# A two-layer spectral convolution: in the mixing stage, the channels' sums and the mixing matmuls alternate in runs of 64 instead of 32

## The chip, the cores and the metric

One Trainium2 chip, of which the kernel uses one core. The metric is the device time of one execution in microseconds (us). The kernel before takes 2893.25 us, the median of three runs (2887.61 to 2897.32).

## The reference

The input x is 16 images of 16 channels of 256 x 256 in fp32. Two layers follow each other, both of the form x + conv(groupnorm(x)).

```python
x = x + _L0_conv_ref(_gn(x), L0_conv_weight)           # 3 x 3 circular convolution, 16 to 16 channels
x = x + _L1_conv_ref(_gn(x), ty, tx, pole1, pole2, residue)
# in _L1_conv_ref
alpha = fft2(x)
A  = 1 / (omega1 - pole1);  Bm = 1 / (omega2 - pole2)
S  = einsum('ikpq,oikp,xikq->oxik', residue, A, Bm)    # a 16 x 16 matrix for each of 256 x 256 frequencies
r1 = einsum('biox,oxik->bkox', alpha, S)               # mix the channels at each frequency
x1 = ifft2(r1).real
x2 = ...                                               # a transient part, from 4 x 4 sums over alpha
return x1 + x2 / Nx / Ny
```

The change concerns S and r1: the matrices S are sums over the poles p and q (here "the channels' sums"), and r1 applies them at each frequency (here "mixing").

## The kernel before

The kernel runs in stages, each with its own buffers. First the 3 x 3 convolution with its statistics (L224 to L284), then the forward transform of each image to half a spectrum, written to the scratch tensor aD in device memory; then the mixing stage (L815 to L1046), which reads aD and writes yD; last the inverse transforms along x and y with the transient part and the output. The change is in the mixing stage alone.

The mixing stage goes through 32 groups g of frequencies along x, each group with four of them and all 256 along the other direction. For each group there are three kinds of work.

- The channels' sums, `sums(kk, w)` (L902): 16 matmuls of 64 rows and 32 columns (array tile 64*32) on 256 columns, from the weights `w` and the constant table `ct`, into two PSUM tiles `ps_s`, the second of them for the odd half of the rows. The matmuls alternate between the two tiles. Eight calls, kk = 0 to 7, make the matrices of a group. Each tile is copied to the tile `sg` in SBUF (L1027), the first of a call by ScalarE and the second by VectorE. There are two `sg` buffers: while group g is mixed out of one, the sums of group g + 1 are written into the other (`ahead`).
- Mixing, `mix(n, sg, yt)` (L958): 8 matmuls with `sg` as the weights (array tile 128*64), on 128 columns of `abd`, the spectrum laid out in blocks, into one PSUM tile `ps_mix`. Sixteen calls make a group; four of them fill one output tile `yt` (L1032), three copied by ScalarE and the fourth by VectorE. Then the quarter of `abd` is loaded for the next group (`load`, L951, four transfers) and `yt` is stored (`store`, L979, four transfers). All of these transfers are issued on the SyncE queue, in program order. `abd` has a buffer for each quarter, `yt` has two buffers.
- The weights of the sums of later groups, `weights(g)` (L858): a generator of three steps. The first does three operations on VectorE (L866 to L873), the second three more with a reciprocal (L875 to L878), the third four (L881 to L884) and then one on GpSimd (L887), and returns the finished tile `wt`.

Each fp32 matmul and its weight load leave two records in the trace, so that 32 matmuls count as 64.

PSUM has eight banks of 128 x 512 fp32. In this stage four belong to `ps_s` (L826) and four to `ps_mix` (L827). A matmul that begins a tile waits until the copy that emptied its bank has ended; which of the four it gets was set at compile time.

The order of the work is written out by hand: the stage runs under `manual_schedule` (L1008), so that each engine executes its instructions as the loop L1016 to L1042 issues them. The loop goes over four quarters n of a group. A quarter is: two calls of `sums` for the next group (32 matmuls), the four copies of their tiles, four calls of `mix` (32 matmuls) with their copies, load, store, and one step of the weights. In the last group (g = 31) there are no sums left. After group 2, `unmix_first` (L986) takes one of the two `yt` buffers to correct the first slot of yD, and gives it back in group 3 after quarter 1.

Of the kernel before, what the change touches and what calls it, by code (L numbers as in the profile page):

```python
# [9 lines left out]
FP = mybir.dt.float32  # L10
# [6 lines left out]
B = 16  # L17
C = 16
N = 256
P = 128  # L20
# [4 lines left out]
def conv_then_laplace_kernel(ctx: ExitStack, tc: tile.TileContext, a: dict, out: bass.AP):  # L25
# [15 lines left out]
    nc = tc.nc  # L41
# [173 lines left out]
    sums = tp.tile([P, 2, B, 12], FP, name="sums", tag="sums")  # L215
# [376 lines left out]
    for g in range(24 * B + 3):  # L592
# [3 lines left out]
        b, n = divmod(g, 24)  # L596
# [24 lines left out]
    def pool(stage, name, bufs=1, **kw):  # L621
        return stage.enter_context(tc.tile_pool(name=name, bufs=bufs, reuse_waits="tile", **kw))
# [17 lines left out]
    m, n = cols[:, 16:17], cols[:, 17:18]  # L640
# [177 lines left out]
    yp = pool(p2, "yt", 2)  # L818
# [10 lines left out]
    def new_sg(g):  # L829
        return (g0, g1)[g % 2].tile([P, N, 2 * C], FP, name="sg", tag="sg")  # L830
# [27 lines left out]
    def weights(g):  # L858

        shape = [P, 32, 4]
        u = up.tile([P, 4, 32, 4], FP, name="u", tag="u")
        w, den, e, f = (u[:, j] for j in range(4))
        pr2, pre, pim = (prU[:, j].unsqueeze(2).to_broadcast(shape) for j in range(3))
        nc.vector.tensor_tensor(  # L866
            w,
            omg[:, g].unsqueeze(1).to_broadcast(shape),
            pims.unsqueeze(2).to_broadcast(shape),
            ALU.subtract,  # L870
        )
        nc.vector.tensor_tensor(den, w, w, ALU.mult)
        nc.vector.tensor_tensor(den, den, pr2, ALU.add)  # L873
        yield
        nc.vector.reciprocal(den, den)  # L875

        nc.vector.scalar_tensor_tensor(e, w, m1, pre, ALU.mult, ALU.add)
        nc.vector.scalar_tensor_tensor(f, w, nm0, pim, ALU.mult, ALU.add)  # L878
        yield
        v = up.tile([P, 32, 2, 2, 4], FP, name="v", tag="v")  # L880
        nc.vector.tensor_tensor(v[:, :, 0, 0], e, den, ALU.mult)  # L881
        nc.vector.tensor_tensor(v[:, :, 1, 1], e, den, ALU.mult)
        nc.vector.tensor_tensor(v[:, :, 1, 0], f, den, ALU.mult)
        nc.vector.tensor_scalar(v[:, :, 0, 1], v[:, :, 1, 0], -1.0, None, ALU.mult)  # L884
        wt = wp.tile([P, 4, 8, 2, 32], FP, name="w", tag="w")
        full = [P, 64, 4, 8]
        nc.gpsimd.tensor_tensor(  # L887
            wt.rearrange("p a k o (i m) -> p (a k o) i m", i=4),
            v.rearrange("p a o r s -> p (a o) (r s)").unsqueeze(2).to_broadcast(full),
            m4.unsqueeze(1).unsqueeze(3).to_broadcast(full),  # L890
            ALU.mult,
        )
        return wt

    def at_once(steps):
        while True:
            try:
                next(steps)
            except StopIteration as e:
                return e.value  # L900

    def sums(kk, w):  # L902

        ps = [pg.tile([P, 2, N], FP, name="ps_s", tag="ps_s") for _ in range(2)]
        for ro in range(2):
            for iq in range(4):
                for odd in range(2):
                    rows = slice(64 * odd, 64 * odd + 64)
                    nc.tensor.matmul(  # L909
                        ps[odd][32 * iq : 32 * iq + 32, ro],  # L910
                        lhsT=w[rows, iq, kk, ro],
                        rhs=ct[rows, iq, kk],
                        start=True,
                        stop=True,
                    )
        return ps

    def first_sums():

        wt, w128 = at_once(weights(0)), at_once(weights(32))
        sg = new_sg(0)
        other = up.tile([P, 2, 2 * C], FP, name="other", tag="other")
        for kk in range(8):
            for h, w in enumerate((wt, w128)):
                fy = slice(P * h, P * h + P)
                ps = sums(kk, w)
                for odd in range(2):
                    k = slice(4 * kk + 2 * odd, 4 * kk + 2 * odd + 2)  # L930
                    copy = (nc.scalar.copy, nc.vector.tensor_copy)[odd]
                    copy(sg[:, fy, k], ps[odd][:, :, fy].rearrange("p r n -> p n r"))
                    copy(other[:, 1 - h, k], ps[odd][:, :, P * (1 - h)])
        for h in range(2):
            o, d = sg[:, P * h], other[:, h]
            nc.vector.tensor_tensor(d, d, o, ALU.subtract)
            nc.vector.scalar_tensor_tensor(o, d, fixrow, o, ALU.mult, ALU.add)
        return sg

    def finish_projections():  # L940


        accs = up.tile([P, 2, B, 16], FP, name="accs", tag="u")
        nc.vector.tensor_tensor(accs, proj[:, :, :, :, 0], proj[:, :, :, :, 1], ALU.add)
        for ro in range(2):
            ps = pm.tile([P, B, 16], FP, name="ps_o", tag="ps_mix")
            nc.tensor.matmul(ps, lhsT=jmat[:, 0], rhs=accs[:, ro], start=True, stop=False)
            nc.tensor.matmul(ps, lhsT=jmat[:, 2 - ro], rhs=accs[:, 1 - ro], start=False, stop=True)
            nc.vector.tensor_copy(o2[:, :, ro], ps)

    def load(g, jq):  # L951
        for s in range(4):
            nc.sync.dma_start(
                out=abd[jq][s::4, s].rearrange("r c j b -> r c (j b)"),
                in_=aD[4 * g + s].rearrange("r (c h n) -> r c h n", c=4, h=4)[:, :, jq],
            )

    def mix(n, sg, yt):  # L958


        ps = pm.tile([P, 4, 2, 4, B], FP, name="ps_mix", tag="ps_mix")
        jq = n // 4
        for j in range(4):
            cc, jj = divmod(4 * (n % 4) + j, 8)
            for t in range(2):
                f = 128 * t + 64 * cc + 16 * jq + 2 * jj
                nc.tensor.matmul(  # L967
                    ps[64 * t : 64 * t + 64, j],
                    lhsT=sg[:, f : f + 2].rearrange("p f m -> p (f m)"),
                    rhs=abd[jq][:, :, 2 * t + cc, 2 * jj : 2 * jj + 2].rearrange(  # L970
                        "p s j b -> p j s b"
                    ),
                    start=True,
                    stop=True,
                )
        j0 = 4 * (n % 4)
        return yt[:, :, :, j0 : j0 + 4], ps.rearrange("p j o s b -> p o (s b) j")

    def store(g, jq, yt):  # L979
        for c in range(4):  # L980
            nc.sync.dma_start(
                out=yD[4 * g : 4 * g + 4, :, c, jq].rearrange("s k n -> k s n"),
                in_=yt[32 * c : 32 * c + 32, c % 2].rearrange("p (s b) j -> p s (b j)", s=4),
            )
# [24 lines left out]
    ahead = first_sums()  # L1009
# [3 lines left out]
    wt = at_once(weights(1))  # L1013
    finish_projections()
    unmix = None
    for g in range(32):  # L1016
        sg, w_now = ahead, wt
        steps = weights(g + 2) if g < 30 else iter(())
        ahead = new_sg(g + 1) if g < 31 else None
        for n in range(4):  # L1020
            evict = []
            if ahead is not None:
                evict = sums(2 * n, w_now) + sums(2 * n + 1, w_now)
            yt = yp.tile([P, 2, 4 * B, 16], FP, name="yt", tag="yt")
            for j, ps in enumerate(evict):
                k = 4 * n + j
                (nc.scalar.copy, nc.vector.tensor_copy)[j % 2](  # L1027
                    ahead[:, :, 2 * k : 2 * k + 2], ps.rearrange("p r n -> p n r")
                )
            for m in range(4):  # L1030
                o, src = mix(4 * n + m, sg, yt)
                (nc.vector.tensor_copy if m == 3 else nc.scalar.copy)(o, src)  # L1032
            if g < 31:
                load(g + 1, n)
            store(g, n, yt)
            if n == 1 and unmix is not None:
                next(unmix, None)
                unmix = None
            try:
                next(steps)  # L1040
            except StopIteration as e:
                wt = wt if e.value is None else e.value  # L1042
        if g == 2:
            unmix = unmix_first()
            next(unmix)
# [152 lines left out]
    for n, (k, b0) in enumerate(units):  # L1198
# [12 lines left out]
        r = rp.tile([P, 2, 4, N], FP, name="r", tag="r")  # L1211
# [163 lines left out]
```

## Time and profile before

From the page of the profile; span 2897.0 us, granted clock 0.965 in the mean over the kernel.

| | busy us | share of the span |
|---|---|---|
| TensorE, matmuls | 2667.3 | 92% |
| TensorE, weight loads | 1971.8 | 68% |
| VectorE | 1940.5 | 67% |
| ScalarE | 1536.0 | 53% |
| GpSimd | 1003.5 | 35% |

| group of instructions | count | busy us | mean ns of one |
|---|---|---|---|
| L967, mixing matmul, 128*64, 128 columns | 8192 | 479.4 | 276 |
| L909, matmul of the sums, 64*32, 256 columns | 8448 | 260.6 | 382 |
| L1027, copy of sums to sg, ScalarE | 248 | 159.9 | 646 |
| L1032, copy of a mix to yt, ScalarE | 384 | 221.6 | 587 |
| L1032, copy of a mix to yt, VectorE | 128 | 88.6 | 692 |

Matmuls of one kind run several at a time in the array, so that the mean of one is longer than the busy time divided by the count. The mixing stage lies between about 1410 and 2130 us of the span, a quarter of the whole. PE is TensorE's matmuls and PEld its weight loads, DVE is VectorE, ACT is ScalarE, SPq the SyncE queue. In a timeline, a line has the start and the length in us, the engine, the line of the kernel, the operation with the tiles it writes and reads, and in brackets the idle time of the engine just before and what ended it.

### The profile page before, as it was taken

How to read it: one execution, taken by the hardware profiler on the slowest of the kernel's cores; microseconds unless marked ns; L12 is line 12 of the kernel's file. 1: busy time of each engine (PE TensorE's matmuls, PEld its weight loads, DVE VectorE, ACT ScalarE, POOL GpSimd, SP SyncE). 2: the span in 40 equal slices, each digit the busy share in tenths (PEclk: the TensorE clock that was granted, in tenths of full speed). 3: DMA queues.
4: the chain of work that ended last, by engine and by line, in shares of the span. 5: the costliest groups of instructions: out<-in, count | busy, mean ns of one | idle time of the engine just before them, and what ended most of it. 6: DMA issues, size and time to landing. Idle time of an engine off the chain costs nothing.

```text
span 2897.0 us, 92787 instructions
## 1 busy us (share of the span) xinstructions
PE 2667.3 (92%) x39536; PEld 1971.8 (68%) x39536; DVE 1940.5 (67%) x3572; ACT 1536.0 (53%) x3098; POOL 1003.5 (35%) x906
## 2 busy tenths in 40 slices
PE   4878878889799999997899999999969999999998
PEld 2333334346577777775688888888868888888887
DVE  7766698886788888887444444444427666766666
ACT  3556677667466666664345555555524444444443
POOL 2232566420233333333211111111135554555553
PEclk9989998899899999998899999999989999999999
DMA  6555667665566666664466666666679999888995
GB/s 257 203 179 187 212 238 256 229 240 192 182 211 211 233 233 224 227 218 169 150 193 191 191 196 193 193 192 191 190 212 312 285 285 288 285 284 285 290 288 188
DMA packets 477335, 650.63 MB, mean 225 GB/s; under 512 B 49065, under 2 KB 458665, under 8 KB 462969
## 3 DMA queue, kind: packets, MB, share of 16 engines
q1 hardware_dynamic: 472920, 635.37, 67.0%
q8 instruction: 312, 5.11, 0.7%
q10 hardware_dynamic: 3408, 7.34, 0.7%
q0 software_dynamic: 592, 1.97, 0.3%
q14 instruction: 103, 0.84, 0.1%
HBM read 365.09 MB, written 279.45 MB: 222 GB/s over the span
## 4 chain that ended last, share of the span: by engine, by line
PE 56%; DMA 9%; DVE 6%; SPq 2%; POOL 1%; issue 1%; ACT 0%; DVEq 0%; ACTq 0%; POOLq 0%
PE ps_mix L967 15%; PE ps_s L909 8%; PE ps_y L678 8%; PE ps_y L686 8%; DMA yk<-yD 4%; PE ps_x L721 4%; PE ps_p L1148 4%; PE ps_f L1157 3%; PE ps_f L1158 3%; DMA out_y<-ol 3%; DVE r L1166 2%; PE psd L706 1%; DVE ol L1168 1%; DVE ol L1169 1%; SPq L1099 1%; DMA yD<-yt 1%
## 5 line engine op out<-in xcount | busy, mean ns | idle before, releaser
L238 PE MATMUL ps_conv<-xt,wc 32*32 32x512 f32 x12288 | 477.4, 641 | 18.0 <-ACT vt L255 11.2
L967 PEld LDWEIGHTS ps_mix<-abd,sg 128*64 128x64 f32 x8192 | 448.5, 138 | 65.5 <-ACT sg L1027 49.8
L967 PE MATMUL ps_mix<-abd,sg 128*64 128x128 f32 x8192 | 479.4, 276 | 13.4 <-ACT yt L1032 13.4
L1112 POOL TENSOR_TENSOR u<-yk 128x512 f32<-128x512 f32 x256 | 342.2, 1366 | 369.8 <-PE ps_p L1148 241.6
L694 ACT ACTIVATE t<-ps_y,vmr 128x384 f32<-128x384 f32 x512 | 297.7, 582 | 168.4 <-PE ps_y L686 157.0
L238 PEld LDWEIGHTS ps_conv<-xt,wc 32*32 32x32 f32 x12288 | 231.8, 106 | 214.8 <-issue 142.1
L1032 DVE COPY yt<-ps_mix 128x512 f32<-128x512 f32 x128 | 88.6, 692 | 363.8 <-PE ps_mix L967 231.8
L678 PE MATMUL ps_y<-tabE,vq 128*128 128x256 f32 x1024 | 313.1, 387 | 13.9 <-DVE vq L667 12.2
L887 POOL TENSOR_TENSOR w<-v,mcol 128x2048 f32<-128x2048 f32 x33 | 119.3, 3614 | 583.8 <-DVE v L884 580.8
L1157 PE MATMUL ps_f<-pt,inv 128*128 128x256 f32 x1024 | 305.8, 380 | 0.0
L686 PE MATMUL ps_y<-tabO,vq 128*128 128x256 f32 x1024 | 305.7, 380 | 0.0
L1158 PE MATMUL ps_f<-hs,ey 128*128 128x256 f32 x1024 | 305.0, 379 | 0.0
L1032 ACT COPY yt<-ps_mix 128x512 f32<-128x512 f32 x384 | 221.6, 587 | 147.2 <-PE ps_mix L967 95.8
L1148 PEld LDWEIGHTS ps_p<-inv,u 128*128 128x128 f32 x2048 | 265.1, 192 | 49.2 <-issue 24.3
L1148 PE MATMUL ps_p<-inv,u 128*128 128x128 f32 x2048 | 278.1, 279 | 12.6 <-POOL u L1115 12.5
L909 PE MATMUL ps_s<-ct,w 64*32 64x256 f32 x8448 | 260.6, 382 | 27.1 <-DMA ct<-cD 27.1
L1161 DVE TENSOR_TENSOR r<-ps_f,q 128x256 f32<-128x256 f32 x256 | 107.2, 419 | 252.1 <-ACT q L1160 252.1
L255 ACT ACTIVATE vt<-ps_conv,xq 128x512 f32<-128x512 f32 x256 | 167.1, 680 | 194.0 <-PE ps_conv L238 193.0
L1027 ACT COPY sg<-ps_s 128x512 f32<-128x512 f32 x248 | 159.9, 646 | 199.7 <-PE ps_s L909 199.5
L678 PEld LDWEIGHTS ps_y<-tabE,vq 128*128 128x128 f32 x1024 | 189.5, 190 | 90.3 <-ACT q L734 50.3
L1160 ACT COPY q<-ps_f 128x256 f32<-128x256 f32 x256 | 95.4, 373 | 290.8 <-PE ps_f L1158 290.8
L909 PEld LDWEIGHTS ps_s<-ct,w 64*32 64x32 f32 x8448 | 158.4, 107 | 92.3 <-POOL abd L1011 27.9
(214 smaller groups left out, 4165.0 us busy)
## 6 DMA issues: line engine op xcount, KB each, us to landing
xt<-in_x SPq DMA_DIRECT2D x32, 2322.0 KB, 9.6
abd<-aD SPq DMA_DIRECT2D x512, 128.0 KB, 3.3
yD<-yt SPq DMA_DIRECT2D x512, 128.0 KB, 2.6
vl<-vD SPq DMA_DIRECT2D x256, 256.0 KB, 3.9
out_y<-ol SPq DMA_DIRECT2D x128, 512.0 KB, 9.8
yk<-yD SPq DMA_DIRECT2D x63, 1024.0 KB, 8.6
s<-vD SPq DMA_DIRECT2D x244, 256.0 KB, 5.9
aD<-spec SPq DMA_DIRECT2D x15, 4096.0 KB, 13.3
```

The lines of the kernel that those rows point to most:

```text
L238: nc.tensor.matmul(acc[r][32 * c : 32 * c + 32], lhsT=ready[b][0][rows, phase, tap], rhs=halves[b][u // 2][rows, q : q + 5 : 4, 2 - tap : ...
L255: nc.scalar.activation(vt[:, r % 2], acc[r], AF.Identity, bias=ready[b][1], **by_sums)
L678: nc.tensor.matmul(ps[:, 0:N], lhsT=vf[:, xo, 0, j], rhs=tabE[:, 0 : i + 2 : i + 1], start=True, stop=False, skip_group_check=True,)
L686: nc.tensor.matmul(ps[:, P : P + N], lhsT=vf[:, xo, 1, j], rhs=tabO[:, i : C + 1 : C - i], start=False, stop=True, skip_group_check=True,)
L694: nc.scalar.activation(t[:, xo, j].rearrange("p l n -> p (l n)"), ps[:, 0:384], AF.Copy, scale=vmr[:, 0, b0 + j, i : i + 1],)
L909: nc.tensor.matmul(ps[odd][32 * iq : 32 * iq + 32, ro], lhsT=w[rows, iq, kk, ro], rhs=ct[rows, iq, kk], start=True, stop=True,)
L967: nc.tensor.matmul(ps[64 * t : 64 * t + 64, j], lhsT=sg[:, f : f + 2].rearrange("p f m -> p (f m)"), rhs=abd[jq][:, :, 2 * t + cc, 2 * jj ...
L1032: (nc.vector.tensor_copy if m == 3 else nc.scalar.copy)(o, src)
L1112: nc.gpsimd.tensor_tensor(u[:, :, j].rearrange("p b (c n) -> p c b n", c=8), in0, in1, o)
L1148: nc.tensor.matmul(ps[:, at], lhsT=u[:, n], rhs=tab, start=True, stop=True)
L1157: nc.tensor.matmul(ps[:, e], lhsT=tab, rhs=pt[:, e], start=True, stop=False)
L1158: nc.tensor.matmul(ps[:, e], lhsT=ey[:, e], rhs=hs, start=False, stop=True)
```

## The change

A group is now gone through in two halves instead of four quarters. A half first makes four calls of `sums` (64 matmuls), each followed by its two copies, and then two quarters of mixing (64 matmuls), with their copies, loads and stores. TensorE thus changes between the two kinds of matmul half as often. Nothing is added to the work or taken from it, and PSUM keeps its four and four banks. The steps of the weights are called five times a group, of which the first three do work: after the sums of the first half, after quarter 0 and after quarter 1.

```diff
         ahead = new_sg(g + 1) if g < 31 else None
-        for n in range(4):
-            evict = []
+        for half in range(2):
             if ahead is not None:
-                evict = sums(2 * n, w_now) + sums(2 * n + 1, w_now)
-            yt = yp.tile([P, 2, 4 * B, 16], FP, name="yt", tag="yt")
-            for j, ps in enumerate(evict):
-                k = 4 * n + j
-                (nc.scalar.copy, nc.vector.tensor_copy)[j % 2](
-                    ahead[:, :, 2 * k : 2 * k + 2], ps.rearrange("p r n -> p n r")
-                )
-            for m in range(4):
-                o, src = mix(4 * n + m, sg, yt)
-                (nc.vector.tensor_copy if m == 3 else nc.scalar.copy)(o, src)
-            if g < 31:
-                load(g + 1, n)
-            store(g, n, yt)
-            if n == 1 and unmix is not None:
-                next(unmix, None)
-                unmix = None
-            try:
-                next(steps)
-            except StopIteration as e:
-                wt = wt if e.value is None else e.value
+                for n in range(4 * half, 4 * half + 4):
+                    for j, ps in enumerate(sums(n, w_now)):
+                        k = 4 * n + 2 * j
+                        (nc.scalar.copy, nc.vector.tensor_copy)[j](
+                            ahead[:, :, k : k + 2], ps.rearrange("p r n -> p n r")
+                        )
+            if half == 0:
+                advance()
+            for n in range(2 * half, 2 * half + 2):
+                yt = yp.tile([P, 2, 4 * B, 16], FP, name="yt", tag="yt")
+                for m in range(4):
+                    o, src = mix(4 * n + m, sg, yt)
+                    (nc.vector.tensor_copy if m == 3 else nc.scalar.copy)(o, src)
+                if g < 31:
+                    load(g + 1, n)
+                store(g, n, yt)
+                if n == 1 and unmix is not None:
+                    next(unmix, None)
+                    unmix = None
+                advance()
```

`advance()` is the `try` of the kernel before, put into a function.

More of the change, by code (lines that the diff above doesn't have):

```diff
@@ L1015, in conv_then_laplace_kernel, with advance @@
     unmix = None
+    def advance():
+        nonlocal wt
+        try:
+            next(steps)
+        except StopIteration as e:
+            wt = wt if e.value is None else e.value
     for g in range(32):
```

## The prediction

> **What bounds the kernel now.** I read four views: the page for the size of the stage, the table of stretches for what is full in it, the chain of waits for the rhythm, and the timeline for who waits for whom at the edges. On the page the mixing matmuls (L967) and the channels' sums (L909) are 479.4 and 260.6 us of TensorE. The table of stretches shows the stage in its steady part (its columns are the length, then PE, PEld, DVE, ACT and POOL busy with counts, the granted clock, the DMA share and GB/s):
>
> ```profile
> 1600.00:1700.00 100.00, 100.00 (x2325) 83.72 (x2304) 48.84 (x103) 55.07 (x91) 14.40 (x4) 1.00 0.68 193
> 1800.00:1900.00 100.00, 100.00 (x2314) 84.05 (x2312) 48.88 (x103) 55.08 (x91) 14.95 (x5) 1.00 0.67 193
> ```
>
> TensorE is never idle and at its full clock; VectorE and ScalarE are half busy. So the stage is bound by TensorE, and any wait put into its stream is paid in full. The chain of waits, in order of time (start, length, what):
>
> ```profile
> 1705.70 3.65 PE ps_mix L967 x64
> 1709.34 1.89 PE ps_s L909 x64
> 1711.23 3.65 PE ps_mix L967 x64
> 1714.88 1.89 PE ps_s L909 x64
> 1716.76 3.64 PE ps_mix L967 x64
> ```
>
> One quarter (32 sums, 32 mixing matmuls, two records each) takes 1.89 + 3.64 = 5.53 us. How much of it is work? In the timeline the two ScalarE copies of successive pairs of sums start at 1478.34 and 1479.20, so a pair costs 0.86 us and the two of a quarter 1.72. Four mixes in a row have their 80 weight loads in 4.35 us (below), 0.0535 us each, so 64 cost 3.42. That is 5.13 us; 0.40 us a quarter is spent at the two changes between the kinds, about 0.17 after the sums and 0.23 after the mixes. The copies out of PSUM (ACT 646, DVE 686 to 692 ns) cost TensorE nothing now: those of the sums lie beside the mixes, and the other way round.
>
> What happens when one kind follows itself is in the trace already. At the end, the last group has no sums, and mixes follow mixes:
>
> ```profile
> 2098.81 4.35 PEld L967 LDWEIGHTS ps_mix<-abd,sg 128*64 128x64 f32 x80 [0.41 <-ACT sg L1027]
> 2102.63 0.69 DVE L1032 COPY yt<-ps_mix 128x512 f32<-128x512 f32 x1 [2.92 <-PE ps_mix L967]
> 2103.38 2.60 PEld L967 LDWEIGHTS ps_mix<-abd,sg 128*64 128x64 f32 x48 [0.22 <-DVE yt L1032]
> ```
>
> After 80 loads (64 of one quarter, 16 of the first mix of the next) the second mix waits for VectorE's copy of the quarter's last mix, and goes on 0.06 us after that copy ends. In the first sums of the stage, pairs of sums follow pairs:
>
> ```profile
> 1389.15 1.65 PEld L909 LDWEIGHTS ps_s<-ct,w 64*32 64x32 f32 x64 [0.19 <-ACT other L933]
> 1390.99 1.65 PEld L909 LDWEIGHTS ps_s<-ct,w 64*32 64x32 f32 x64 [0.19 <-ACT other L933]
> ```
>
> Two pairs take 1.84 us instead of 1.72: with four banks, the third pair waits for the copies of the first, though these are short there (0.42 and 0.15 us).
>
> **What the skill says.** TensorEngine Tiling (Array Packing), section Tiling Modes, Key Properties: changing the tiling mode, not just the tile, drains TensorE. The trace agrees: 64*32 and 128*64 are two modes, and the two changes cost 0.40 us together, whatever else is going on. The same page, section Performance Considerations, PSUM Bottleneck: packing speeds up the matmuls, not the copies out of PSUM, which can become the limit. It agrees in the two places just shown. TensorE: Matmul & The Clock Gate, the table at its head: VectorE and ScalarE take their work strictly in order. The trace agrees: at 1720.51 VectorE copies a mix, then runs four operations on the weights, and only then, at 1721.98, the copy of the sums that was ready at about 1721.57.
>
> **The change, part by part.** *Removed:* in each group with sums (31 of them) eight changes of mode become four. Two pairs of changes at 0.40 us: 0.80 us a group, 24.8 us in all. All of it is on the path, since TensorE is the path.
>
> *Unchanged:* the number of matmuls, copies, loads, stores and their sizes. The weights' steps for group g + 2 are three calls a group in both; in the changed kernel they come after the first half's sums, after quarter 0 and after quarter 1. The first two lie on VectorE beside mixes and are hidden (0.9 and 1.5 us in front of a copy that is due more than 2 us later). The third is not, below.
>
> *Added, a: mixes behind mixes.* Both PSUM pools have four banks, and a quarter's four mixes take all four. The compiled order gives the second mix of the odd quarter the bank of the fourth mix of the even one, which VectorE empties, as at the end of the kernel before. Copy starts 0.41 us after the fourth mix's last issue (2102.63 against 2098.81 + 64 x 0.0535 = 2102.23), takes 0.69, wake 0.06: 1.16 us. In that time only the first mix of the odd quarter can run, 0.86. Wait: 0.30 us. The idle entry of the row shows 0.22, the largest value by adding is 0.36. Waits on ScalarE's banks end earlier. In the compiled order 59 of the 62 half groups have this bank: 59 x 0.30 = 17.7 us.
>
> *Added, b: sums behind sums, first half.* Eight tiles of sums in four banks: the third pair takes the banks of the first. In a quarter where VectorE has no weights to do (1477.15), its copy starts 1.23 us after the first sums and takes 0.71: end at 1.94, plus 0.06 is 2.00. The pair could start at 1.72. Wait: 0.28 us. The fourth pair needs copies that end at 2.09 + 0.70 = 2.79, and is due at 2.86: none. Bounds: 0.12, as in the first sums with their shorter copies, to 0.40. 31 x 0.28 = 8.7 us.
>
> *Added, c: sums behind sums, second half.* Here VectorE's queue holds, in this order: the copy of quarter 1's last mix, the four operations of the third step (L881 to L884, some 0.95 us), and the copy of the first pair of sums. That is the order of this stretch of the kernel before, where nobody waits for it because mixes come next:
>
> ```profile
> 1720.34 1.96 PE L909 MATMUL ps_s<-ct,w 64*32 64x256 f32 x64
> 1720.51 0.69 DVE L1032 COPY yt<-ps_mix 128x512 f32<-128x512 f32 x1 [2.35 <-PE ps_mix L967]
> 1721.12 0.28 DVE L881 TENSOR_TENSOR v<-u 128x128 f32<-128x128 f32 x1
> 1721.84 0.23 DVE L884 TENSOR_SCALAR v<-v 128x128 f32<-128x128 f32 x1
> 1721.98 1.28 DVE L1027 COPY sg<-ps_s 128x512 f32<-128x512 f32 x2
> ```
>
> The copy starts 1.64 us after the first sums, takes 0.69, and the odd half of the third pair goes on about 0.1 later: 2.43 against 1.72. Wait: 0.71 us. Bounds: 0.55, if the first matmuls of the pair, which need ScalarE only, run ahead, to 1.0, if the copy starts later. Behind this copy are those of the second pair (end 2.95, due 3.3) and, much later, of the mixes: nobody else waits. The last group with sums has no weights to make: 30 x 0.71 + 0.28 = 21.6 us.
>
> *Moved, d: one place.* After group 2 a tile of scratch takes one of the two output buffers (L990). The kernel before idles there for a store, 1.08 and 2.23 us of TensorE. With quarters 0 and 1 back to back, quarter 1's copies wait for quarter 0's store, and the sums' copies wait behind them; I take 3 us more (0 to 6).
>
> *Stores and loads.* They are 16 a half group instead of 8 a quarter, on one queue, which is already taken up almost without a gap: from 1704.40 to 1709.81 it issues eight in 5.4 us. The second quarter's store then ends about when its buffer is wanted again, within a few tenths. A late buffer delays ScalarE's first copy of a quarter; it has 0.27 us to spare a mix, and 1.1 us before the next sums' copy. I cost it at nothing.
>
> Sum: -24.8 + 17.7 + 8.7 + 21.6 + 3 = +26.2 us. 2893.25 + 26 = 2919.5 us.
>
> **Rivals.** *The waits are hidden, faster:* only the changes of mode count, 2893 - 25 = 2868; with a third of the waits, 2893 - 25 + 16 = 2884. For it: VectorE and ScalarE are half idle. Against it: both tails above show TensorE stopped by just these banks, with copies no slower. 6%.
> *A draw:* half of the waits, 2893 - 25 + 24 + 1 = 2893. For it: the waits are differences of larger numbers, and 0.1 us in each of the four of a group is 12 us in all. Against: three of the four were measured in this trace. 13%.
> *The store queue as well:* if the second quarter's copies wait for a store for so long that the next sums' copies are late, 0.5 us a half group, 62 x 0.5 = 31 more: 2950. For it: the queue is near full, and two buffers make each store due soon. Against: the slower rhythm (5.7 to 5.8 us a quarter) gives it more time, not less. 10%.
> *As worked out,* 71%.
>
> **How the numbers follow.** The likeliest case gives 2919.5. Its own bounds: a 13 to 21, b 4 to 12, c 17 to 30, d 0 to 6, gain 20 to 25, so from +9 to +49; both ends at once are unlikely. The range 2898 to 2942 leaves out the faster case, part of the draw and the upper part of the store case, about 2 in 10. Faster by 0.3% (under 2884.6) 6%, within it 13%, slower 81%.
>
> **What would show it.** In the profile after: the chain of waits in stretches of some 7.4 us of mixes and 3.9 to 4.5 us of sums; a group at about 22.9 us instead of 22.1; TensorE's idle time before L967 put down to VectorE's yt, 0.2 to 0.3 us some 59 times, and before L909 to the sg copies, larger in every second half. The 0.41 us entries before L967 halve in number. I am wrong on the gain if the changes of mode that remain cost more than 0.40 a pair, on the waits if TensorE's idle time in the steady part is under 0.8 us a group, and on the stores if ScalarE's yt copies wait over 1 us for yD in most groups.

## The result, and the profile after

The changed kernel takes 2920.8 us in the median (2919.18 to 2923.68, four runs) against 2894.4 before, which is now the median of four runs: a ratio of 1.0096, with a 95% interval of 1.0076 to 1.0116. It is slower by 26.4 us; 26.2 was worked out.

The table of stretches of the changed kernel, with the columns of the prediction's first fence:

```profile
1600.00:1700.00 100.00, 99.90 (x2250) 81.78 (x2236) 49.70 (x99) 54.11 (x87) 14.40 (x4) 1.00 0.66 189
```

TensorE still counts as busy all the time, at its full clock, but it gets 2250 matmul records into the 100 us and not 2325: it is slower for the same work. Its busy share of 99.90 us in 100 doesn't show why. The chain of waits does:

```profile
1701.37 4.27 PE ps_s L909 x128
1705.64 7.33 PE ps_mix L967 x128
1712.97 1.89 PE ps_s L909 x64
1714.86 0.02 issue
1714.88 1.96 PE ps_s L909 x64
1716.84 7.33 PE ps_mix L967 x128
```

A group is 4.27 + 7.33 + 3.87 + 7.33 = 22.80 us, and 26 groups from 1507.85 to 2100.61 us took 22.80 each. Before, 26 groups from 1504.36 to 2080.33 us took 22.15 each. Where the long runs are longer than they need be is in the timeline of the same stretch:

```profile
1701.30 1.48 PEld L909 LDWEIGHTS ps_s<-ct,w 64*32 64x32 f32 x64 [0.17 <-issue]
1701.48 0.69 DVE L1042 COPY yt<-ps_mix 128x512 f32<-128x512 f32 x1 [1.71 <-PE ps_mix L967]
...
1702.81 0.23 DVE L884 TENSOR_SCALAR v<-v 128x128 f32<-128x128 f32 x1
1702.95 1.28 DVE L1033 COPY sg<-ps_s 128x512 f32<-128x512 f32 x2
...
1703.15 0.13 PEld L909 LDWEIGHTS ps_s<-ct,w 64*32 64x32 f32 x2 [0.38 <-ACT sg L1033]
...
1703.69 1.47 PEld L909 LDWEIGHTS ps_s<-ct,w 64*32 64x32 f32 x62 [0.40 <-DVE sg L1033]
...
1705.57 4.35 PEld L967 LDWEIGHTS ps_mix<-abd,sg 128*64 128x64 f32 x80 [0.41 <-DMA abd<-aD]
...
1710.13 2.60 PEld L967 LDWEIGHTS ps_mix<-abd,sg 128*64 128x64 f32 x48 [0.22 <-DVE yt L1042]
...
1714.88 0.62 PEld L909 LDWEIGHTS ps_s<-ct,w 64*32 64x32 f32 x32 [0.50 <-DVE sg L1033]
...
1715.74 0.62 PEld L909 LDWEIGHTS ps_s<-ct,w 64*32 64x32 f32 x32 [0.25 <-DVE sg L1033]
```

All three waits for banks that the prediction named are there. In the second half's sums VectorE copies a mix, makes the weights' third step up to L884, and comes to the sums only at 1702.95, 1.65 us after they began; TensorE stops after the 64th load, does two more when ScalarE's copy has ended, and goes on at 1703.69, when the first of VectorE's two has. In the mixes it stops after 80 loads for VectorE's yt. In the first half's sums it stops after 64 loads again, until 1714.88, and once more until 1715.74. The entries of 0.41 us before L967 (here put down to a load of abd) are read as the change of mode, as before.

The place after group 2 is in the chain too, and is longer than before:

```profile
1481.02 2.28 DMA yD<-yt
...
1484.03 5.38 PE ps_mix L967 x64
1489.41 2.00 PE ps_s L909 x64
...
1491.49 0.69 DVE yt L1042
1492.18 0.66 DVE z L997
...
1495.43 0.23 DVE v L884
1495.66 0.61 DVE sg L1033
...
1496.31 2.55 PE ps_s L909 x32
```

Group 3 lasts from 1474.31 to 1507.92, 33.6 us, 10.8 more than its neighbours. In the kernel before it was 27.2, from 1477.20 to 1504.41, 5.1 more than its neighbours.

### The profile page after: what moved, and what is told of

It is laid out like the page before. It is cut to its first block, busy times and chain, and to the rows that moved or that the text cites. A ratio compares the mean times of both kernels' runs of the same rounds, so it can differ in the third digit from the quotient of the medians.

```text
span 2917.4 us, 92756 instructions
## 1 busy us (share of the span) xinstructions
PE 2684.2 (92%) x39536; PEld 1974.1 (68%) x39536; DVE 1951.2 (67%) x3572; ACT 1542.0 (53%) x3098; POOL 1004.1 (34%) x906
## 3 DMA queue, kind: packets, MB, share of 16 engines
q0 software_dynamic: 592, 1.97, 0.3%
## 4 chain that ended last, share of the span: by engine, by line
PE 55%; DMA 10%; DVE 6%; SPq 2%; POOL 1%; issue 1%; ACT 0%; DVEq 0%; ACTq 0%; POOLq 0%
PE ps_mix L967 16%; PE ps_s L909 9%; PE ps_y L678 8%; PE ps_y L686 8%; DMA yk<-yD 6%; PE ps_x L721 4%; PE ps_p L1155 3%; PE ps_f L1164 3%; PE ps_f L1165 3%; DVE r L1173 3%; DMA out_y<-ol 2%; SPq L1106 2%; PE psd L706 1%; DVE ol L1175 1%; DVE ol L1176 1%; PE ps_h L1139 1%
## 5 line engine op out<-in xcount | busy, mean ns | idle before, releaser
L967 PE MATMUL ps_mix<-abd,sg 128*64 128x128 f32 x8192 | 479.8, 276 | 10.9 <-ACT yt L1042 10.9
L238 PE MATMUL ps_conv<-xt,wc 32*32 32x512 f32 x12288 | 469.9, 632 | 18.5 <-ACT vt L255 11.1
L967 PEld LDWEIGHTS ps_mix<-abd,sg 128*64 128x64 f32 x8192 | 451.2, 138 | 50.5 <-DMA abd<-aD 17.7
L887 POOL TENSOR_TENSOR w<-v,mcol 128x2048 f32<-128x2048 f32 x33 | 119.2, 3613 | 602.5 <-DVE v L884 599.5
L909 PE MATMUL ps_s<-ct,w 64*32 64x256 f32 x8448 | 274.9, 383 | 31.3 <-DMA ct<-cD 27.0
L909 PEld LDWEIGHTS ps_s<-ct,w 64*32 64x32 f32 x8448 | 159.9, 107 | 127.5 <-DVE sg L1033 35.7
L1033 ACT COPY sg<-ps_s 128x512 f32<-128x512 f32 x248 | 168.0, 678 | 147.7 <-PE ps_s L909 147.0
```

The lines of the kernel that those rows point to most:

```text
L238: nc.tensor.matmul(acc[r][32 * c : 32 * c + 32], lhsT=ready[b][0][rows, phase, tap], rhs=halves[b][u // 2][rows, q : q + 5 : 4, 2 - tap : ...
L909: nc.tensor.matmul(ps[odd][32 * iq : 32 * iq + 32, ro], lhsT=w[rows, iq, kk, ro], rhs=ct[rows, iq, kk], start=True, stop=True,)
L967: nc.tensor.matmul(ps[64 * t : 64 * t + 64, j], lhsT=sg[:, f : f + 2].rearrange("p f m -> p (f m)"), rhs=abd[jq][:, :, 2 * t + cc, 2 * jj ...
L1033: (nc.scalar.copy, nc.vector.tensor_copy)[j](ahead[:, :, k : k + 2], ps.rearrange("p r n -> p n r"))
```

## The experiments

The theory is the prediction's: fewer changes of mode are a gain, and the longer runs wait for PSUM banks. The rivals are that the changes of mode cost something else than was read out of the trace, and that the loss lies in the stores and the two output buffers. The waits for yD did grow, as the list of who waited for whom in the steady part of the changed kernel shows (us in all, times, longest):

```profile
DVE yt L1042 <- DMA yD<-yt: 112.3, 45, 2.9
ACT yt L1042 <- DMA yD<-yt: 70.9, 38, 3.3
```

Before, these were 57.7 and 19.7 us, 20 and 24 times.

### The third step of the weights after the second half's sums

```diff
-            if half == 0:
-                advance()
+            advance()
             for n in range(2 * half, 2 * half + 2):
...
-                advance()
+                if n != 1:
+                    advance()
```

> The changed kernel, with the third step of the weights (L881 to L887) issued after the copies of the second half's sums and not ahead of them. Theory (the loss is waits for PSUM banks): the second half's run of sums falls from 4.27 us to the first half's 3.87, 0.40 us in 30 groups, 12 us: 2909. Rival (the loss is in the stores and the output buffers, whose waits in the trace have grown): no change, 2921. If the step were needed early for the next group's sums, 2925 or more.

Measured: 2904.6 us, 16 less than the changed kernel. The chain of waits has the same short run in both halves:

```profile
1704.97 1.89 PE ps_s L909 x64
1706.86 0.02 issue
1706.87 1.97 PE ps_s L909 x64
```

The second half's run fell from 4.27 to 3.88, 0.39 us in 30 groups, 12 us as expected. The other 4 us are mostly in group 3, which takes 30.3 us here and not 33.6. There VectorE's work on the first slot is no longer followed by the third step ahead of the copies of the sums; that step is 0.9 of these 3.3 us, and the rest was not traced. So the wait behind VectorE's queue is shown. The stores can't explain the gain: ScalarE waited longer for yD here, 99.6 us in the steady part for 70.9.

### VectorE copies the second mix and not the fourth

```diff
-                    (nc.vector.tensor_copy if m == 3 else nc.scalar.copy)(o, src)
+                    (nc.vector.tensor_copy if m == 1 else nc.scalar.copy)(o, src)
```

> The changed kernel, with VectorE copying the second of the four mixes of a quarter and ScalarE the other three; before it was the fourth. In the compiled order each mix then gets the bank of the same mix of the quarter before. Theory: the wait of mixes behind mixes goes, 0.28 us 59 times, 16.5 us; and VectorE has nothing to wait for ahead of the third step, which ends before the second half's sums are done, 12 us more: 2892, runs of mixes at 7.05 us, runs of sums at 3.87 in both halves. Rival (stores): 2921. Rival (ScalarE becomes late for the sums, as it now has the fourth mix): runs of sums longer than 3.87, 2900 or more.

Measured: 2898.3 us, 22 less than the changed kernel, 1.0019 of the kernel before (1.0011 to 1.0028). The chain of waits:

```profile
1713.37 3.86 PE ps_s L909 x128
1717.23 7.14 PE ps_mix L967 x128
```

One digit in the code takes away the wait between the mixes (7.33 to 7.14) and the one behind the third step (4.27 to 3.86). The runs of sums are as expected. The runs of mixes are not at 7.05: the wait between them was taken for 0.28 us and was 0.19, and 0.09 us 59 times are 5 of the 6 us by which the time misses 2892. A group is 22.0 us, just less than the 22.15 of before, and the kernel is still no faster than before: its group 3 takes 32.1 us (1471.52 to 1503.64), 10.1 more than its neighbours, where before it was 5.1.

The same edit on the kernel before:

> The kernel before, with VectorE copying the second of the four mixes, as in vector_takes_second_mix. Theory: with runs of 32 no bank is wanted early, so who copies which mix is of no account: 2893, quarters of 1.89 and 3.64 us. Rival (the edit is good in itself, whatever the runs): 2875 to 2885, as the changed kernel gained some 22 us by it.

Measured: 2891.1 us, 0.9992 (0.9981 to 1.0003), with quarters of 1.89 and 3.64 us. So who copies which mix matters only where mixes follow mixes.

### Runs of 16

```diff
-            evict = []
-            if ahead is not None:
-                evict = sums(2 * n, w_now) + sums(2 * n + 1, w_now)
...
+            for part in range(2):
+                if ahead is not None:
+                    for j, ps in enumerate(sums(2 * n + part, w_now)):
...
+                for m in range(2 * part, 2 * part + 2):
```

> The kernel before, with sums and mixes alternating by 16 (one pair of sums, two mixes): eight pairs of changes of mode in a group and not four, nothing else moved; no bank is wanted early. Theory (a pair of changes costs 0.40 us): 31 groups of four more, 49.6 us: 2944. Rival (the 0.40 us of a quarter is not the change of mode but something that a quarter has once): 2894. If changing costs less for shorter runs, between.

Measured: 2925.3 us, 32 more than before and not 50. The chain of waits alternates without any wait:

```profile
1701.11 1.02 PE ps_s L909 x32
1702.14 1.90 PE ps_mix L967 x32
```

With 16 and 32 matmuls there are two points on a line for each kind. Sums: 1.02 and 1.89, so 0.87 a pair and 0.15 a run. Mixes: 1.90 and 3.64, so 0.87 a mix and 0.16 a run. A pair of changes of mode costs 0.31 us, not 0.40. The four more in a group are 1.23 us (23.38 us a group against 22.15), 38 us in 31 groups. The stage did grow by so much in the traces, by 39 us from the first sums of group 0 to the last mixes of group 30. The 6 us that the measured 32 are short of it lie outside the stage, where the traces differ: its first sums start at 1401.73 us here and at 1409.96 before.

### Six banks for the sums, two for the mixes

This kernel has two edits more: VectorE copies the second mix, as above, and the correction of the first slot has its own scratch, as in the next section.

```diff
-    pg = pool(p2, "p_s", 4, space=PSUM)
-    pm = pool(p2, "p_mix", 4, space=PSUM)
+    pg = pool(p2, "p_s", 6, space=PSUM)
+    pm = pool(p2, "p_mix", 2, space=PSUM)
```

> As vector_second_own_scratch, with six banks for the sums and two for the mixes. Only the fourth pair of sums reuses banks, those of the first, long empty. Theory: runs of sums fall from 3.87 to 2 x 1.89 - 0.15 = 3.63 us, which is the wait b of 0.24 us by itself; runs of mixes grow from 7.14 to some 7.7 to 8.2, as each mix waits for the copy of the last but one. Rival (the 0.24 us is a property of long runs of sums and not a wait for a bank): sums stay at 3.87.

Measured: 2927.9 us in one run, of which only the lengths in the trace are used. The timeline of TensorE:

```profile
1613.26 3.69 PE L909 MATMUL ps_s<-ct,w 64*32 64x256 f32 x128
1616.88 5.69 PE L967 MATMUL ps_mix<-abd,sg 128*64 128x128 f32 x96
```

From the first sum to the first mix it is 1616.88 - 1613.26 = 3.62 us; 3.63 was worked out. So the 0.25 us that are left in the run of 3.87 are a wait for a bank, and the run of 4.27 waits 0.65. The mixes grew to 7.68 us (1605.58 to 1613.26) in a good half, and to more where they also stood behind late stores, and cost more than the sums gained.

### The place after group 2

Without the correction of the first slot:

```diff
-        if g == 2:
-            unmix = unmix_first()
-            next(unmix)
```

> The changed kernel without the correction of the first slot (unmix_first is left out, so that part of the output is not corrected): no output buffer is taken away after group 2. Theory: group 3 takes 22.8 us and not 33.6, 10.8 us less: 2910. Rival (the buffers are short all the time): less than 3 us, 2918 or more.

Measured: 2907.8 us, 13 less than the changed kernel. Where group 3 was, the groups go on in equal steps of 22.8 us.

The correction can also have its own scratch, in memory that is free at that time (the projections' tile and the weights' v tile; its arithmetic is rewritten to need less), with its second part after quarter 3. On the kernel before:

```diff
-        z2 = yp.tile([P, 2, 4, 256], FP, name="z2", tag="yt")
+        z = proj.rearrange("p h b m s -> p (h b m s)").rearrange("p (c n) -> p c n", c=4)
...
+        t = up.tile([P, 2, 256], FP, name="t", tag="v")
...
-            if n == 1 and unmix is not None:
+            if n == 3 and unmix is not None:
```

> The kernel before, with the scratch of the first slot's correction in the memory of the projections, which are done with by then, and in the weights' v tile, so that no output buffer is taken away; the second part comes after quarter 3. Theory: group 3 takes 22.15 us and not 27.2: 5 us less, 2888. Rival (the correction is hidden): 2893.

Measured: 2889.5 us, 0.9991 (0.9982 to 0.9999), 4 us less than before. That these are the 5 us of the place is not shown: in the trace groups 3 and 4 are together still 4.2 us longer than their neighbours (24.81 and 23.68 us), and the chain of waits still goes through stores there. The place costs 11 us in the changed kernel by the trace, and 13 by leaving the correction out; the 5 us of the kernel before are the length of its group 3 alone.

### What is left when the waits are gone

The changed kernel with VectorE on the second mix and the correction's own scratch, the two diffs above:

> The changed kernel with VectorE copying the second mix and the correction's own scratch. Theory: what is left is the gain of two pairs of changes of mode less the wait of sums behind sums in both halves, 22.0 us a group against 22.12 before, 31 x 0.12 = 4 us, and 5 us for group 3: 2884. Rival (the stores hold ScalarE up): 2893 or more.

Measured: 2893.0 us, 1.0001 (0.9990 to 1.0012). Some 9 us are missing, though the group is 22.0 us where nothing disturbs it. In the trace groups 3 and 4 are together 5.5 us longer than that (1468.70 to 1518.27), and their chain goes through two stores that landed late; the groups after them lost 3 us in single late runs of sums. So the own scratch takes away about half of the place's 10.1 us, and the expectation counted on all of them. With five banks for the sums and three for the mixes, in the same two lines as for six and two:

> As vector_second_own_scratch, with five PSUM banks for the sums and three for the mixes instead of four and four. In the compiled order the first tile of the third pair of sums has a bank that is free, the second waits for ScalarE's copy of the first pair, about 0.1 us less than now. Theory: runs of sums fall from 3.87 to about 3.77, runs of mixes stay at 7.14, 62 x 0.1 = 6 us less: 2878. Rival (three banks are too few for the mixes): runs of mixes over 7.14, and 2884 or more.

Measured: 2906.4 us, slower by 13 and not faster by 6. The run of sums did fall, to 3.82. The timeline shows what took the time:

```profile
1703.90 1.99 SPq L981 DMA_DIRECT2D yD<-yt  x4
1704.37 1.07 ACT L1045 COPY yt<-ps_mix 128x512 f32<-128x512 f32 x2 [3.18 <-DMA yD<-yt]
...
1705.00 0.85 PEld L967 LDWEIGHTS ps_mix<-abd,sg 128*64 128x64 f32 x16 [2.07 <-ACT yt L1045]
```

ScalarE waits 3.18 us for a store to give it an output buffer, and with three banks the mixes stand still behind it; over the steady part that is 18.2 us of idle TensorE, where with four banks there was none before the mixes. The stores, which the prediction costed at nothing, do reach TensorE once the slack in PSUM is used for something else. To test this, the queue was relieved: the loads of abd, which nobody needs for a whole group, go to GpSimd's queue, and SyncE issues the stores alone.

```diff
-            nc.sync.dma_start(
+            nc.gpsimd.dma_start(
                 out=abd[jq][s::4, s].rearrange("r c j b -> r c (j b)"),
```

> As vector_second_own_scratch (2893.0), with the loads of abd issued on GpSimd's queue, so that SyncE's has the stores alone and issues each as soon as its copies are done. Theory (what was missing there, 2893 for 2884, are output buffers that wait for late stores): ScalarE's yt copies no longer wait for yD, and the time is 2884, as worked out there. Rival (the missing part is elsewhere, as in a stage before or after): 2893, with the waits gone. If GpSimd's issuing disturbs VectorE, more than 2893.

Measured: 2883.6 us, 0.9965 (0.9951 to 0.9978). Nobody waits for yD in the steady part any more, and the 9 us are there. Some 7 of them are seen in the trace: groups 3 and 4 are 1.1 us too long and not 5.5, and the late runs after them lose 0.4 us and not 3. Whether the stores had been late because the queue was full or because they stood behind loads that wait for the mixes isn't separated by this.

> As all_with_five_and_three_banks (2906.4), with the loads of abd on GpSimd's queue. Theory: that kernel lost its time where the mixes, with three banks, stood behind copies that waited for a store; with the stores issued in time they run in 7.14 us, the sums in 3.82, and a group takes 21.9 us: 2881, the fastest so far. Rival (three banks are too few in themselves): 2900 or more.

Measured: 2879.5 us, 0.9954 (0.9940 to 0.9968), faster than the kernel before and the changed one. Its interval overlaps with that of the last run, so that the change of banks is not shown to add to the gain. The chain of waits:

```profile
1707.26 3.82 PE ps_s L909 x122
1711.08 7.14 PE ps_mix L967 x128
```

A group takes 21.9 us. The same on the kernel before with its own scratch went the other way:

> The kernel before with the correction's own scratch (2889.5) and with the loads of abd on GpSimd's queue. Theory: with runs of 32 and four banks the late stores cost nothing, so nothing is gained: 2889. Rival (the queue costs the kernel before as well): 2880 to 2885.

Measured: 2906.4 us, 17 more than without. Who waited for whom in its steady part:

```profile
PE ps_s L909 <- POOL w L887: 18.0, 25, 2.9
```

GpSimd also makes the last operation of the weights (L887, 3.6 us). In the kernel before the third step comes after quarter 2, and on GpSimd behind quarter 2's loads, which wait for the mixes; the next group's sums then wait for the weights, and once in nearly every group TensorE stands for 0.7 us. In the changed kernel the step comes a quarter earlier and has the time. So how much of the 2879.5 is owed to the longer runs and how much to the queue alone can't be read off a pair of runs; the faster rhythm of the groups, 22.15 to 21.92 us, accounts for 7 us of the 10 between it and the 2889.5 of the kernel before with its own scratch.

## Why the prediction was right, and which of its terms were not

The bound was right: TensorE alone sets the pace of the stage, every wait in its stream was paid, and VectorE and ScalarE, half idle, were late all the same. The places of the waits were right, bank by bank. In us a group:

| term | predicted | measured | from |
|---|---|---|---|
| two pairs of changes of mode fewer | -0.80 | -0.62 | 2 x 0.31, runs of 16 and of 32 |
| a, mixes behind mixes, twice | +0.60 | +0.38 | 7.33 - 7.14, twice |
| b, sums behind sums, first half | +0.28 | +0.25 | 3.87 - 3.62 |
| c, sums behind sums, second half | +0.71 | +0.65 | 4.27 - 3.62 |
| sum | +0.79 | +0.66 | 22.80 - 22.15 = 0.65 in the trace |
| d, the place after group 2, once | +3 | +5.7 | 10.8 - 5.1 |

That the sum fell so near is partly luck. The gain was taken too large by 0.18 us a group, the waits by 0.31, and the one place too small by 2.7 us; 31 x 0.66 + 5.7 = 26.2 us is the same figure again.

Part of it is one slip that enters twice, with opposite signs.

- *The gain* was mis-sized in "80 weight loads in 4.35 us (below), 0.0535 us each". These 80 are the loads of five mixes, and 4.35 / 80 is 0.0544 us. The 64 of a quarter are then 3.48 us, and the two changes 0.33 and not 0.40. Runs of 16 and 32 give 0.87 us a mix, the same figure, and 0.87 a pair of sums where the prediction took 0.86; this leaves 0.31. A difference of nearly equal numbers wants two run lengths, not one.
- *a* has the same slip. With 0.0544 the copy starts 0.34 us after the fourth mix's last load and not 0.41, the first mix of the odd quarter takes 0.87, and the wait comes out at 0.22, which is what the idle entry shows. The stream of matmuls lost 0.19. The count of 59 is in the trace as well: the three of the 62 half groups that the compiled order leaves out start their mixes at 1410.13, 1421.49 and 1511.71 us and take 7.14 us for them, in the changed kernel as it stands.
- *b, c* held within 0.06 us. The measured copy at 1.65 us after the first sums is the predicted 1.64. The sign given for them, idle entries before L909 that are larger in every second half, did not come: they are 0.50 + 0.25 us in the first half and 0.38 + 0.40 in the second, while the runs differ by 0.40. The Trainium skill (TensorE: Matmul & The Clock Gate, the table at its head) says that TensorE pulls weight loads ahead of running matmuls, and the trace agrees: in the run of sums with six banks the 128 loads were done in 3.20 us and the matmuls in 3.69. So a part of the loads' idle time is only their lead, lost: of the 0.75 us in the first half the matmuls lost 0.25. What a wait costs is read from the lengths of the runs.
- *d* was inside its bounds, near the upper one. Its mechanism is in the chain: the copies of quarter 1 wait for a store until 1491.49 (put down to the sums here, and to yD in the same place of the kernel with the later step), and those of the sums stand behind them. What it left out is that VectorE then does its five operations of the correction and the third step, up to 1495.66, before it copies the first sums; for these the matmuls stood 1.13 us more, in part the wait that c counts in every group. No experiment separates the correction's part, so the 2.7 us are open.
- *Stores at nothing* held for the steady part of the changed kernel: its groups have the four run lengths above to 0.01 us, and no idle time before L967 is put down to late ScalarE copies. Yet the prediction's own sign of being wrong on them came: ScalarE's yt copies waited over 1 us for yD in 26 of 27 groups between 1510 and 2110 us, before in 6. The sign was badly chosen, as a late copy that no bank is wanted from costs TensorE nothing. For a better version the term would not have held: of the kernel without these waits, the late stores took 9 us.

## What to carry to other kernels

Here runs of one kind of matmul could only be lengthened as far as there were banks for them: with four banks a run of four pairs waits for the copies of its own first pair, and a change of mode saved (0.15 us each) is soon less than a copy waited for (0.19 to 0.65 us). Before alternating more coarsely, look at which engine copies the last tile of a run, and at what stands ahead of the first tile's copy on that engine's queue; here moving one copy to an earlier mix was worth 22 us. And slack hides more than one thing: when it is used up, look again at the waits that cost nothing before.

## What had not been expected

- What a run costs beyond its matmuls, read as the change of tiling mode at its end, is nearly the same for both kinds, 0.15 us for the sums and 0.16 for the mixes, although the weight loads' idle entries are 0.41 and 0.17.
- The SyncE queue was the hidden second limit. The four loads of a quarter took it 2.45 us at least and the four stores 1.97, of the 5.7 us that a quarter has. Only with the loads on another queue (0.55 us each on GpSimd), beside the two edits before, did the kernel with fewer changes of mode become a faster one.
- A move between queues isn't neutral: the same edit gained 9 us in one order of the work and lost 17 in the other, for the order of the weights' third step on GpSimd.
